# A Perceiver block's cross-attentions: the context taken by 512 keys in one piece, in place of two pieces of 256

## The chip, the cores and the metric

The kernel runs on one core of a Trainium2 chip. The metric is the device time of one execution in microseconds (us); lower is better. The core has five engines that run side by side and meet at semaphores: TensorE (PE in the profile, with its weight loads as PEld), VectorE (DVE), ScalarE (ACT), GpSimd (POOL) and SyncE (SP), which here issues the transfers between the chip's main memory and the on-chip memory SBUF. Matrix products land in a second on-chip memory, PSUM.

## The reference, cut to what matters

The model is a Perceiver of four layers on two sequences (b = 0, 1) of 256 rows and 256 features. Each layer is a cross-attention to a context of 4096 rows per sequence, then a self-attention, then a feed-forward block:

```python
x = x + _L0_xattn_ref(_layernorm(x, axis=-1), ctx_1024, mask_BxS2_bk0, ...)   # one head, masked
x = x + _L0_attn_ref(...);  x = x + _L0_ffn_ref(...)
x = x + _L1_xattn_ref(_layernorm(x, axis=-1), ctx_1024, ctx_1024, ...)        # one head
x = x + _L1_attn_ref(...);  x = x + _L1_ffn_ref(...)
x = x + _L2_xattn_ref(_layernorm(x, axis=-1), ctx_1024, ...)                  # one head
x = x + _L2_attn_ref(...);  x = x + _L2_ffn_ref(...)
x = x + _L3_xattn_ref(_layernorm(x, axis=-1), ctx_1024, mask_BxS2_ik0, ...)   # 16 heads
x = x + _L3_attn_ref(...);  x = x + _L3_ffn_ref(...)
```

The first three cross-attentions have one head of 256 features. Each is softmax(q k^T) v over 4096 keys, for 256 queries of each sequence. In layer 0 some keys are masked.

## The kernel before, in words

**One-head cross-attention** (`xattn_mean`, called by `xattn`). The key projection is folded into the queries and the value projection is done after the mean, so scores are taken straight from the context: 256 queries against the transposed context `ctxT`, and the weighted mean of the context rows `ctx`. It runs six times, for n = 0, 1, 2 and b = 0, 1. The 4096 keys are walked in 8 units of `UN` = 512 keys; a unit has two steps, one for each half q of 128 queries, so a call has 16 steps.

For exactness near fp32 every operand of a product is a pair h + l: h is the value rounded by ScalarE in a copy to fp32r, l is the rest, from a subtraction. `mm3` (L405) makes one product of a pair by a pair with three matmuls.

A unit's context comes in four transfers of 256 KB: two halves of `CK` = 256 keys of `ctxT` (L715) and two of `ctx` (L717), into buffers `raw`, of which there are 6. `parts` splits each half: h by ScalarE (L725), l by POOL (L727) or DVE (L729). The table `POOL` (L1790) says which: of the keys `kx` the first half goes to DVE and the second to POOL; of the values `vx` both go to POOL. `KV_BUFS` (L1789) gives four half-size buffers to each of `kx` and `vx`, that is two units.

Step i does the following, in this order of writing:

- `scores(i)`: splits of the next unit (keys at q = 0, values at q = 1, then the fetch of the unit after), and the score products into one PSUM bank `s`: for each half h of the keys and each half c of the features one `mm3`, so 12 matmuls of 256 columns (L405, tile xs).
- `turn(i - 1)`: four transposes of the previous step's exponentials on PE (L777), and their h part on ScalarE (L779).
- `greatest(i)`: for n = 0 a predicated copy on DVE that overwrites masked scores in PSUM (L756, with the mask `gone` and the value `fill` in SBUF), then the greatest score of each row on DVE (L758) and a running minimum of its negative (L760).
- the l part of the transposed exponentials on DVE (L780).
- `exponents(i)`: the exponential on ScalarE (L766), the scale of the older sums (L768, L771).
- `values(i - 2)`: 12 matmuls of 256 columns (L405, tile xmm<-xvx,xpT) and the running sum on DVE (L792, L793).

All these but the splits and transfers are tied by `Turns` to the order of writing on each engine. The splits, the transfers, and the work of other stages are placed among them by the framework's scheduler, which fixes one static order for each engine. Every engine and SP's queue then run in that order: an instruction that waits holds those behind it.

**What runs beside it.** There are two lanes. The x lane holds the cross-attentions; the a lane holds the self-attentions and feed-forward blocks of the other sequence, whose weights come as 128x1024 tiles (512 KB) and are split in the same way: h on ScalarE (L395), l on POOL (L397) or DVE (L399) by turns.

**Preparation for layer 3** (`prep`, `prep_alone`). Keys and values of layer 3's 16 heads are projected from the same split context and stored to main memory. `PREP` (L1785) has ten units prepared within cross-attentions, from the pieces that these hold; the other six are done by `prep_alone`, which fetches and splits pieces of 256 keys itself, with the buffers of `KV_BUFS` in its first use, ahead of the first cross-attention, and with two elsewhere.

Of the kernel before, what the change touches and what calls it, by code (L numbers as in the profile page):

```python
# [18 lines left out]
F32 = mybir.dt.float32  # L19
# [9 lines left out]
P = 128  # L29
# [603 lines left out]
class Perceiver:  # L633
# [51 lines left out]
    def xattn_mean(self, xp, n, b, queries):  # L685

        k, nc = self.x, self.nc  # L690
        masked = n == 0
        n_u, n_h, n_t = L // self.UN, self.UN // self.CK, self.UN // P
        qkT, qb, fill = queries
        ctxT = self.ins["ctxT"].rearrange("(c p) n -> p c n", p=P)
        prep = self.PREP.get((n, b), ())
        if prep:
            w3 = k.weights("x3.wk", "x3.wv")
        tie = Turns(self.tc).put
        raw, kx, vx, gone, score, exps, turned = {}, {}, {}, {}, {}, {}, {}


        least, most, total, o = ([None, None] for _ in range(4))

        def fetch(u):
            if masked:
                gone[u] = k.t(xp, [P, self.UN], "gone", U8, bufs=3)
                at = u * self.UN
                nc.sync.dma_start(gone[u], self.gone_d[b : b + 1, at : at + self.UN].to_broadcast([P, self.UN]))
            for name in ("kx", "vx"):
                raw[name, u] = []  # L710
                for h in range(n_h):
                    at = b * L + u * self.UN + h * self.CK
                    r = k.t(xp, [P, 2, self.CK], "raw", bufs=self.KV_BUFS["raw"])
                    if name == "kx":
                        nc.sync.dma_start(r, ctxT[:, :, at : at + self.CK])  # L715
                    else:
                        nc.sync.dma_start(r, self.ins["ctx"][at : at + self.CK, :].rearrange("(k p) d -> p k d", p=P))  # L717
                    raw[name, u].append(r)

        def parts(name, got, u):  # L720
            got[u] = []
            for h, r in enumerate(raw.pop((name, u))):
                both = k.t(xp, [P, 2, 2, self.CK], name, F32R, bufs=self.KV_BUFS[name])
                x = Pair(both[:, 0], both[:, 1])
                nc.scalar.copy(x.h, r)  # L725
                if self.POOL[name][h]:
                    nc.gpsimd.tensor_tensor(x.l, r, x.h.bitcast(F32), ALU.subtract)  # L727
                else:
                    nc.vector.tensor_sub(x.l, r, x.h)  # L729
                got[u].append(x)  # L730

        def scores(i):
            u, q = divmod(i, 2)
            if i == 0:
                fetch(0)
                parts("kx", kx, 0)
                parts("vx", vx, 0)
                fetch(1)
            if u + 1 < n_u:
                if q == 0:  # L740
                    parts("kx", kx, u + 1)
                else:
                    parts("vx", vx, u + 1)
                    if u + 2 < n_u:
                        fetch(u + 2)
            score[i] = k.t(k.ps, [P, self.UN], "s")
            for h in range(n_h):
                for c in range(2):
                    k.mm3(score[i][:, h * self.CK : (h + 1) * self.CK], qkT[:, c, q * P : (q + 1) * P], kx[u][h][:, c, :], c == 0, c == 1, tie)
            if q == 1 and u in prep:  # L750
                self.prep(xp, b, u, kx[u], *w3)

        def greatest(i):
            u, q = divmod(i, 2)
            if masked:
                tie(nc.vector.copy_predicated(score[i], gone[u], fill[:, q : q + 1].to_broadcast([P, self.UN])))  # L756
            nm = k.t(k.sm, [P, 1], f"nm{q}")
            tie(nc.vector.tensor_reduce(nm, score[i], axis=AX.X, op=ALU.max, negate=True))  # L758
            if u:
                tie(nc.vector.tensor_scalar(nm, nm, least[q], None, ALU.min))  # L760
            least[q] = nm

        def exponents(i):
            u, q = divmod(i, 2)
            p, su = k.t(xp, [P, self.UN], "p", bufs=2), k.t(k.sm, [P, 1], f"su{q}", bufs=4)
            tie(nc.scalar.activation(p, score.pop(i), AF.Exp, bias=least[q], accum_out=su))  # L766
            top, down = k.t(k.sm, [P, 1], f"top{q}"), None
            tie(nc.vector.tensor_scalar(top, least[q], -1.0, qb[:, q : q + 1], ALU.mult, ALU.add))  # L768
            if u:
                down = k.t(k.sm, [P, 1], f"down{q}")  # L770
                tie(nc.scalar.activation(down, top, AF.Exp, bias=most[q], scale=-1.0))  # L771
            most[q], exps[i] = top, (p, su, down)

        def turn(i):
            p, pst = exps[i][0], k.t(k.ps, [P, 512], "mm")
            for t in range(n_t):
                tie(nc.tensor.transpose(pst[:, t * P : (t + 1) * P], p[:, t * P : (t + 1) * P], self.eye))  # L777
            turned[i] = k.t2(xp, [P, self.UN], "pT", bufs=2)
            tie(nc.scalar.copy(turned[i].h, pst))  # L779
            return lambda: tie(nc.vector.tensor_sub(turned[i].l, pst, turned[i].h))  # L780

        def values(i):
            u, q = divmod(i, 2)
            (_, su, down), pT = exps.pop(i), turned.pop(i)
            acc = k.t(k.ps, [P, 512], "mm")[:, :D]
            for t in range(n_t):
                k.mm3(acc, pT[:, t * P : (t + 1) * P], vx[u][t // 2][:, t % 2, :], t == 0, t == n_t - 1, tie)
            if u == 0:
                o[q], total[q] = k.t(xp, [P, D], f"o{q}", bufs=1), su
                tie(nc.vector.tensor_copy(o[q], acc))  # L790
            else:
                tie(nc.vector.tensor_scalar(su, total[q], down, su, ALU.mult, ALU.add))  # L792
                tie(nc.vector.scalar_tensor_tensor(o[q], o[q], down, acc, ALU.mult, ALU.add))  # L793
                total[q] = su

        steps = 2 * n_u
        for i in range(steps + 2):
            rest = lambda: None
            if i < steps:
                scores(i)  # L800
            if 1 <= i <= steps:
                rest = turn(i - 1)
            if i < steps:
                greatest(i)
            rest()
            if i < steps:
                exponents(i)
            if i >= 2:
                values(i - 2)
        ps = k.mm2()  # L810
        for q in range(2):
            r = k.t(k.sm, [P, 1], "ur")
            nc.vector.reciprocal(r, total[q])
            nc.vector.tensor_scalar(o[q], o[q], r, None, ALU.mult)
            for c in range(2):
                nc.tensor.transpose(ps[:, c, q * P : (q + 1) * P], o[q][:, c * P : (c + 1) * P], self.eye)
        oT = k.t2(xp, [P, 2, S], "kvk", bufs=2)
        k.split(oT, ps)
        return oT
# [17 lines left out]
    def prep_alone(self, xp, b, units, bufs=None):  # L837
# [6 lines left out]
        for u in units:  # L844
            kx = []
            for h in range(self.UN // self.CK):
                at = b * L + u * self.UN + h * self.CK
                both = k.t(xp, [P, 2, 2, self.CK], "kx", F32R, bufs=bufs or self.KV_BUFS["kx"])
                kx.append(Pair(both[:, 0], both[:, 1]))
                raw = k.t(xp, [P, 2, self.CK], "raw", bufs=bufs or self.KV_BUFS["raw"])  # L850
                nc.sync.dma_start(raw, ctxT[:, :, at : at + self.CK])
                k.split(kx[h], raw, lo=nc.gpsimd)
            k.mm_tags = ["mm", "mm", "pr"]
# [3 lines left out]
    def prep(self, xp, b, u, kx, wk, wv, bufs=2):  # L857

        k, nc = self.x, self.nc
        for m in range(2):  # L860
            ps = k.mm()
            for h, x in enumerate(kx):
                for d in range(2):
                    k.mm3(ps[:, h * self.CK : (h + 1) * self.CK], wk[d][:, m * P : (m + 1) * P], x[:, d, :], d == 0, d == 1)
            kk = k.t2(xp, [P, self.UN], "kvk", bufs=bufs)
            k.split(kk, ps, k.col("x3.bk", m))
            for dst, part in ((self.kh_d, kk.h), (self.kl_d, kk.l)):
                nc.sync.dma_start(dst[b, u, :HD, 8 * m : 8 * m + 8, :].rearrange("d h n -> h d n"), part.bitcast(F32))
        v = k.t(xp, [P, 4, self.UN // P, GRP, HD + 1], "kvv", bufs=1)
        nc.gpsimd.memset(v[:, :, :, :, HD], 1.0)  # L870
        for h, x in enumerate(kx):
            ps = k.mm2()
            for t in range(2):
                for d in range(2):
                    k.mm3(ps[:, t, :], x[:, d, t * P : (t + 1) * P], wv[d], d == 0, d == 1)
            for t in range(2):
                k.copy(v[:, :, 2 * h + t, :, :HD], ps[:, t, :].rearrange("p (g j d) -> p g j d", g=4, j=GRP))
        nc.sync.dma_start(self.v_d[b, :, :, u, :].rearrange("g p n -> p g n"), v.rearrange("p g k j r -> p g (k j r)"))
# [907 lines left out]

    ALONE = {}
    FIRST, BEFORE, BEHIND = (0, 2), (2, 4), (4, 6)
    KV_BUFS = {"kx": 4, "vx": 4, "raw": 6}  # L1789
    POOL = {"kx": (0, 1), "vx": (1, 1)}  # L1790

    @contextmanager
    def psum(self, lane, **tags):
# [132 lines left out]
```

## Time and profile before

| what | value |
|---|---|
| median of 3 runs (lowest, highest) | 1585.57 us (1581.46, 1586.45) |
| the profiled execution's own time | 1590.7 us |
| its span, first to last instruction | 1588.9 us |
| mean granted TensorE clock | 0.916 |
| busy share of the span: PE, DVE, ACT, POOL | 87%, 70%, 56%, 34% |

The steps of the six cross-attentions, by the starts of their first and last row maximum (L758):

| call | first, us | last, us |
|---|---|---|
| n = 0, b = 0 | 35.4 | 95.1 |
| n = 0, b = 1 | 97.6 | 172.7 |
| n = 1, b = 0 | 345.8 | 472.7 |
| n = 1, b = 1 | 476.0 | 581.8 |
| n = 2, b = 0 | 603.9 | 667.2 |
| n = 2, b = 1 | 715.5 | 797.7 |

How to read the profile: times are from one execution. A row of a group has the line, the engine, the operation, the tiles written and read by the program's names, the shapes, how many there were, and their durations. Matmuls follow each other in a pipeline, so their durations overlap; what one costs in a row of them is the distance from start to start. A timeline row has the start, the length, the engine, the line and the operation, and in brackets how long the engine was idle before it and what ended that. The table of windows gives each engine's busy time in a stretch.

### The profile page before, as it was taken

The page shows a single profiled execution, that of the slowest core. Times are in us where ns is not written, and L with a number is a line of the kernel's source. Part 1 is how long each engine was busy: PE and PEld are TensorE (multiplying, and loading weights), DVE is VectorE, ACT ScalarE, POOL GpSimd, SP SyncE. Part 2 cuts the span into 40 slices and gives each one's busy share as a digit, 9 for nine tenths or more (in the row PEclk, how much of TensorE's full clock was granted, in tenths as well). Part 3 has the DMA queues.
Part 4 walks back from the last instruction along what each step waited for, and adds up shares of the span by engine and source line. Part 5 has one row for each costly group of instructions (what it writes and reads, how often), then busy time and mean ns, then how long its engine had stood idle before and what let it go on. Part 6 is the DMA issues. An engine that isn't in the chain of part 4 may idle for free.

```text
span 1588.9 us, 29546 instructions
## 1 busy us (share of the span) xinstructions
PE 1387.5 (87%) x11278; PEld 1126.0 (71%) x11278; DVE 1106.4 (70%) x1895; ACT 891.8 (56%) x1669; POOL 534.7 (34%) x395
## 2 busy tenths in 40 slices
PE   6899798978999998989973679979999999888498
PEld 6898688968899998988973245645555554774387
DVE  6999755455577787865663666759999980566764
ACT  5676455556866656745631016648888889233242
POOL 6655244444455454663354000120000000530441
PEclk9999899979999999999996558879999999996699
DMA  8753165564556575546454512456676741200471
GB/s 292 224 150 115 51 177 172 187 192 160 166 160 207 161 217 162 160 143 187 134 143 122 85 59 57 111 131 114 113 116 111 114 71 31 85 1 3 175 254 35
DMA packets 126628, 212.32 MB, mean 134 GB/s; under 512 B 14212, under 2 KB 90532, under 8 KB 122964
## 3 DMA queue, kind: packets, MB, share of 16 engines
q1 hardware_dynamic: 126488, 210.45, 48.7%
q8 instruction: 89, 1.46, 0.4%
q14 instruction: 51, 0.42, 0.1%
HBM read 181.72 MB, written 29.01 MB: 133 GB/s over the span
## 4 chain that ended last, share of the span: by engine, by line
PE 46%; DVE 16%; DMA 9%; ACT 4%; POOL 3%; issue 2%; SPq 1%; DVEq 0%; ACTq 0%; POOLq 0%
PE amm L405 9%; PE xacc L573 7%; DVE xpm L1375 6%; PE xmm L405 5%; PE xf L1369 5%; PE xs L405 4%; PE xpr L405 3%; DMA awr<-in_w 3%; PE amm L1396 2%; DMA xk<-akh_d 2%; PE xs L1396 2%; PE amm L1756 2%; PE xmm L777 1%; PE amm L573 1%; POOL aw L397 1%
## 5 line engine op out<-in xcount | busy, mean ns | idle before, releaser
L1375 DVE TENSOR_REDUCE xpm<-xf 128x2 f32<-128x1024 f32 x232 | 281.7, 1222 | 34.2 <-PE xf L1369 31.9
L397 POOL TENSOR_TENSOR aw<-awr,aw 128x1024 fp32r<-128x1024 f32 (+1 forms) x61 | 145.7, 2390 | 299.8 <-ACT aw L395 294.0
L1397 ACT ACTIVATE xp<-amm 128x512 f32<-128x512 f32 x299 | 170.1, 595 | 31.0 <-PE amm L1396 17.9
L395 ACT CAST aw<-awr 128x1024 fp32r<-128x1024 f32 (+1 forms) x114 | 115.5, 1016 | 116.0 <-DMA awr<-in_w 69.5
L405 PE MATMUL xmm<-xvx,xpT 128*128 128x256 f32 x1152 | 167.0, 291 | 4.5 <-DVE xpT L780 2.5
L573 PE MATMUL xacc<-xp,xv 128*17 128x256 f32 x2048 | 165.7, 397 | 0.9 <-DVE xot L591 0.9
L405 PE MATMUL xs<-xkx,xqkT 128*128 128x256 f32 x1152 | 164.0, 286 | 1.4 <-POOL xkx L727 0.6
L727 POOL TENSOR_TENSOR xvx<-xraw,xvx 128x512 fp32r<-128x512 f32 x96 | 131.6, 1387 | 82.9 <-ACT xvx L725 72.1
L405 PEld LDWEIGHTS xmm<-xvx,xpT 128*128 128x128 f32 x1152 | 147.7, 193 | 8.0 <-issue 3.7
L405 PEld LDWEIGHTS xs<-xkx,xqkT 128*128 128x128 f32 x1152 | 149.2, 193 | 3.5 <-POOL xkx L727 1.0
L1397 ACT ACTIVATE xp<-xs 128x512 f32<-128x512 f32 x213 | 123.5, 595 | 37.1 <-PE xs L1396 22.5
L1369 PE MATMUL xf<-xk,xq 49*128 49x512 f32 x464 | 125.4, 530 | 15.8 <-DVE xpm L1375 6.9
L1369 PEld LDWEIGHTS xf<-xk,xq 49*128 49x128 f32 x464 | 46.7, 195 | 114.4 <-issue 79.8
L399 DVE TENSOR_TENSOR aw<-awr,aw 128x1024 fp32r<-128x1024 f32 (+1 forms) x53 | 81.2, 1533 | 66.5 <-ACT aw L395 66.2
L405 PE MATMUL amm<-axnT,aw 128*128 128x256 f32 x648 | 101.1, 313 | 11.7 <-ACT axnT L395 6.9
L405 PEld LDWEIGHTS amm<-axnT,aw 128*128 128x128 f32 x648 | 92.3, 216 | 20.3 <-ACT axnT L395 9.7
L405 PE MATMUL amm<-ah,aw 128*128 128x256 f32 x768 | 99.3, 285 | 6.6 <-ACT au L1002 3.3
L1396 PE MATMUL amm<-xq,xk 51*128 51x256 f32 x598 | 99.6, 297 | 4.2 <-DVE aqT L393 2.9
L727 POOL TENSOR_TENSOR xkx<-xraw,xkx 128x512 fp32r<-128x512 f32 x48 | 72.3, 1506 | 89.8 <-ACT xkx L725 89.7
L405 PEld LDWEIGHTS amm<-ah,aw 128*128 128x128 f32 x768 | 94.3, 191 | 9.3 <-ACT au L1002 3.9
L1420 POOL TENSOR_TENSOR ax<-ax,ax 128x128 f32<-128x128 f32 x8 | 3.7, 458 | 281.8 <-DVE ax L603 281.8
L1396 PEld LDWEIGHTS amm<-xq,xk 51*128 51x128 f32 x598 | 83.9, 188 | 18.2 <-issue 12.6
(545 smaller groups left out, 2918.0 us busy)
## 6 DMA issues: line engine op xcount, KB each, us to landing
awr<-in_w SPq DMA_DIRECT2D x106, 512.0 KB
xraw<-in_ctxT SPq DMA_DIRECT2D x108, 256.0 KB
xraw<-in_ctx SPq DMA_DIRECT2D x96, 256.0 KB
xk<-akh_d SPq DMA_DIRECT2D x128, 128.0 KB
av_d<-xkvv SPq DMA_DIRECT2D x16, 544.0 KB
xv<-av_d SPq DMA_DIRECT2D x32, 272.0 KB
akh_d<-xkvk SPq DMA_DIRECT2D x32, 256.0 KB
akl_d<-xkvk SPq DMA_DIRECT2D x32, 256.0 KB
```

The source lines that it names most:

```text
L395: nc.scalar.copy(dst.h, src)
L397: lo.tensor_tensor(dst.l, src, dst.h.bitcast(F32), ALU.subtract)
L399: nc.vector.tensor_sub(dst.l, src, dst.h)
L405: tie(self.nc.tensor.matmul(out, lhsT=x, rhs=y, start=start and i == 0, stop=stop and i == 2))
L573: inst = self.nc.tensor.matmul(acc[STRIP * j : STRIP * j + v(j).shape[1], :S], lhsT=v(j), rhs=p[:, j, :], start=start, stop=stop)
L727: nc.gpsimd.tensor_tensor(x.l, r, x.h.bitcast(F32), ALU.subtract)
L777: tie(nc.tensor.transpose(pst[:, t * P : (t + 1) * P], p[:, t * P : (t + 1) * P], self.eye))
L1369: tie(nc.tensor.matmul(ps[h], lhsT=q4[rows, j, t * P : (t + 1) * P], rhs=k4[rows, j, :], start=True, stop=True))
L1375: nc.vector.tensor_reduce(at, both.rearrange("p (h n) -> p h n", h=2), axis=AX.X, op=ALU.max)
L1396: tie(nc.tensor.matmul(ps[h][:, j, :], lhsT=ks[c][rows, a + j, s * P : (s + 1) * P], rhs=q4[rows, a + j, :], start=True, stop=True))
L1397: exps = [nc.scalar.activation(p[:, h, a : a + 2, :], ps[h], AF.Exp, scale=0.25) for h in range(2)]
L1756: nc.tensor.matmul(ps[:, f, :], lhsT=w1[half][:, c, f * P : (f + 1) * P], rhs=buf[:, c, e * cap : (e + 1) * cap], start=c == 0, stop=c == 1)
```

## The change

A unit's 512 keys are one piece. There are two transfers of 512 KB for a unit in place of four of 256 KB; `raw` has 3 buffers of twice the size; each piece is split by one ScalarE copy of 128x1024 and one subtraction of 128x1024, on DVE for keys and on POOL for values, with 2 buffers of a whole unit. The score products have 512 columns: 6 matmuls a step in place of 12. `prep` takes one piece of 512 or two of 256 keys. `prep_alone` still takes pieces of 256, and its first use now has 2 buffers for splits and 3 for raw pieces, where it had 4 and 6. Line numbers after the change: scalar copy L717, POOL subtraction L719, DVE subtraction L721, predicated copy L746, row maximum L748, exponential L756.

```diff
         def fetch(u):
+            at = b * L + u * self.UN
             if masked:
...
-            for name in ("kx", "vx"):
-                raw[name, u] = []
-                for h in range(n_h):
-                    at = b * L + u * self.UN + h * self.CK
-                    r = k.t(xp, [P, 2, self.CK], "raw", bufs=self.KV_BUFS["raw"])
...
+            r = raw["kx", u] = k.t(xp, [P, 2, self.UN], "raw", bufs=3)
+            nc.sync.dma_start(r, ctxT[:, :, at : at + self.UN])
+            r = raw["vx", u] = k.t(xp, [P, 2 * self.UN], "raw", bufs=3).rearrange("p (k d) -> p k d", k=n_t)
+            nc.sync.dma_start(r, self.ins["ctx"][at : at + self.UN, :].rearrange("(k p) d -> p k d", p=P))
 
         def parts(name, got, u):
-            got[u] = []
-            for h, r in enumerate(raw.pop((name, u))):
-                both = k.t(xp, [P, 2, 2, self.CK], name, F32R, bufs=self.KV_BUFS[name])
-                x = Pair(both[:, 0], both[:, 1])
-                nc.scalar.copy(x.h, r)
-                if self.POOL[name][h]:
-                    nc.gpsimd.tensor_tensor(x.l, r, x.h.bitcast(F32), ALU.subtract)
-                else:
-                    nc.vector.tensor_sub(x.l, r, x.h)
-                got[u].append(x)
+            r = raw.pop((name, u))
+            got[u] = x = k.t2(xp, list(r.shape), name, bufs=2)
+            nc.scalar.copy(x.h, r)
+            if name == "vx":
+                nc.gpsimd.tensor_tensor(x.l, r, x.h.bitcast(F32), ALU.subtract)
+            else:
+                nc.vector.tensor_sub(x.l, r, x.h)
...
-            for h in range(n_h):
-                for c in range(2):
-                    k.mm3(score[i][:, h * self.CK : (h + 1) * self.CK], qkT[:, c, q * P : (q + 1) * P], kx[u][h][:, c, :], c == 0, c == 1, tie)
+            for c in range(2):
+                k.mm3(score[i], qkT[:, c, q * P : (q + 1) * P], kx[u][:, c, :], c == 0, c == 1, tie)
             if q == 1 and u in prep:
-                self.prep(xp, b, u, kx[u], *w3)
+                self.prep(xp, b, u, [kx[u]], *w3)
...
-                k.mm3(acc, pT[:, t * P : (t + 1) * P], vx[u][t // 2][:, t % 2, :], t == 0, t == n_t - 1, tie)
+                k.mm3(acc, pT[:, t * P : (t + 1) * P], vx[u][:, t, :], t == 0, t == n_t - 1, tie)
...
-                both = k.t(xp, [P, 2, 2, self.CK], "kx", F32R, bufs=bufs or self.KV_BUFS["kx"])
+                both = k.t(xp, [P, 2, 2, self.CK], "kx", F32R, bufs=bufs or 2)
...
-                raw = k.t(xp, [P, 2, self.CK], "raw", bufs=bufs or self.KV_BUFS["raw"])
+                raw = k.t(xp, [P, 2, self.CK], "raw", bufs=bufs or 3)
...
-                    k.mm3(ps[:, h * self.CK : (h + 1) * self.CK], wk[d][:, m * P : (m + 1) * P], x[:, d, :], d == 0, d == 1)
+                    k.mm3(ps[:, h * n : (h + 1) * n], wk[d][:, m * P : (m + 1) * P], x[:, d, :], d == 0, d == 1)
...
-    KV_BUFS = {"kx": 4, "vx": 4, "raw": 6}
-    POOL = {"kx": (0, 1), "vx": (1, 1)}
```

More of the change, by code (lines that the diff above doesn't have):

```diff
@@ L691, in xattn_mean @@
         masked = n == 0
-        n_u, n_h, n_t = L // self.UN, self.UN // self.CK, self.UN // P
+        n_u, n_t = L // self.UN, self.UN // P
         qkT, qb, fill = queries
@@ L704, in fetch @@
         def fetch(u):
+            at = b * L + u * self.UN
             if masked:
                 gone[u] = k.t(xp, [P, self.UN], "gone", U8, bufs=3)
-                at = u * self.UN
-                nc.sync.dma_start(gone[u], self.gone_d[b : b + 1, at : at + self.UN].to_broadcast([P, self.UN]))
-            for name in ("kx", "vx"):
-                raw[name, u] = []
-                for h in range(n_h):
-                    at = b * L + u * self.UN + h * self.CK
-                    r = k.t(xp, [P, 2, self.CK], "raw", bufs=self.KV_BUFS["raw"])
-                    if name == "kx":
-                        nc.sync.dma_start(r, ctxT[:, :, at : at + self.CK])
-                    else:
-                        nc.sync.dma_start(r, self.ins["ctx"][at : at + self.CK, :].rearrange("(k p) d -> p k d", p=P))
-                    raw[name, u].append(r)
-        def parts(name, got, u):
-            got[u] = []
-            for h, r in enumerate(raw.pop((name, u))):
-                both = k.t(xp, [P, 2, 2, self.CK], name, F32R, bufs=self.KV_BUFS[name])
-                x = Pair(both[:, 0], both[:, 1])
-                nc.scalar.copy(x.h, r)
-                if self.POOL[name][h]:
-                    nc.gpsimd.tensor_tensor(x.l, r, x.h.bitcast(F32), ALU.subtract)
-                else:
-                    nc.vector.tensor_sub(x.l, r, x.h)
-                got[u].append(x)
+                nc.sync.dma_start(gone[u], self.gone_d[b : b + 1, at - b * L :][:, : self.UN].to_broadcast([P, self.UN]))
+            r = raw["kx", u] = k.t(xp, [P, 2, self.UN], "raw", bufs=3)
+            nc.sync.dma_start(r, ctxT[:, :, at : at + self.UN])
+            r = raw["vx", u] = k.t(xp, [P, 2 * self.UN], "raw", bufs=3).rearrange("p (k d) -> p k d", k=n_t)
+            nc.sync.dma_start(r, self.ins["ctx"][at : at + self.UN, :].rearrange("(k p) d -> p k d", p=P))
+        def parts(name, got, u):
+            r = raw.pop((name, u))
[5 more added lines that the diff above has]
+                nc.vector.tensor_sub(x.l, r, x.h)
         def scores(i):
@@ L861, in prep @@
             ps = k.mm()
+            n = self.UN // len(kx)
             for h, x in enumerate(kx):
                 for d in range(2):
-                    k.mm3(ps[:, h * self.CK : (h + 1) * self.CK], wk[d][:, m * P : (m + 1) * P], x[:, d, :], d == 0, d == 1)
+                    k.mm3(ps[:, h * n : (h + 1) * n], wk[d][:, m * P : (m + 1) * P], x[:, d, :], d == 0, d == 1)
             kk = k.t2(xp, [P, self.UN], "kvk", bufs=bufs)
@@ L870, in prep @@
         nc.gpsimd.memset(v[:, :, :, :, HD], 1.0)
-        for h, x in enumerate(kx):
+        for h in range(2):
             ps = k.mm2()
             for t in range(2):
+                x, at = kx[(2 * h + t) * P // n], (2 * h + t) * P % n
                 for d in range(2):
-                    k.mm3(ps[:, t, :], x[:, d, t * P : (t + 1) * P], wv[d], d == 0, d == 1)
+                    k.mm3(ps[:, t, :], x[:, d, at : at + P], wv[d], d == 0, d == 1)
             for t in range(2):
```

## The prediction

> **What bounds the kernel now.** I read the engines' busy slices first, then a table of windows over the six cross-attentions, then the timeline of one unit. The 40 slices of the span and the windows say which engine sets the pace where:
>
> ```profile
> PE   6899798978999998989973679979999999888498
> DVE  6999755455577787865663666759999980566764
> ...
> 75.00:100.00 25.00, 24.00 (x199) 23.24 (x198) 22.80 (x54) 18.87 (x45) 17.33 (x12) 1.00 0.55 160
> 125.00:150.00 25.00, 22.99 (x167) 21.40 (x168) 23.27 (x48) 15.75 (x36) 15.90 (x11) 1.00 0.41 128
> 150.00:175.00 25.00, 22.56 (x171) 21.73 (x169) 23.70 (x52) 14.13 (x34) 11.07 (x8) 0.93 0.15 47
> 500.00:525.00 25.00, 25.00 (x215) 25.00 (x214) 22.23 (x48) 17.47 (x39) 14.74 (x11) 1.00 0.56 163
> 625.00:650.00 25.00, 25.00 (x213) 24.85 (x212) 20.84 (x49) 19.05 (x43) 16.36 (x12) 1.00 0.48 149
> ```
>
> (A window's columns: PE, PEld, DVE, ACT, POOL busy us, clock, DMA share, GB/s.) In the masked layer 0 (to 175 us) DVE is busy 91 to 95% of the time and PE has gaps; in layers 1 and 2 (500, 625) PE is packed and DVE has some air. So DVE work counts in the first, PE work in the second. One masked unit:
>
> ```profile
> 80.25 0.70 DVE L756 COPY_PREDICATED xs<-xgone,xfill 128x512 f32<-128x512 uint8 x1 [0.28 <-PE xs L405]
> 80.86 0.68 DVE L729 TENSOR_TENSOR xkx<-xraw,xkx 128x512 fp32r<-128x512 f32 x1
> 81.46 0.68 DVE L758 TENSOR_REDUCE xnm<-xs 128x1 f32<-128x512 f32 x1
> 82.18 0.21 DVE L760 TENSOR_SCALAR xnm<-xnm,xnm 128x1 f32<-128x1 f32 x1
> ...
> 83.60 0.90 DVE L756 COPY_PREDICATED xs<-xgone,xfill 128x512 f32<-128x512 uint8 x1
> ...
> 87.08 0.70 DVE L756 COPY_PREDICATED xs<-xgone,xfill 128x512 f32<-128x512 uint8 x1 [0.33 <-PE xs L405]
> ```
>
> ```profile
> 80.99 1.70 POOL L727 TENSOR_TENSOR xkx<-xraw,xkx 128x512 fp32r<-128x512 f32 x1 [2.13 <-ACT xkx L725]
> 82.65 2.99 POOL L727 TENSOR_TENSOR xvx<-xraw,xvx 128x512 fp32r<-128x512 f32 x2
> ```
>
> The unit lasts 87.08 - 80.25 = 6.83 us, with 0.33 us of DVE idle. The second predicated copy takes 0.90 us and not 0.70, while POOL subtracts. Two more places show what that is:
>
> ```profile
> 51.58 2.53 POOL L727 TENSOR_TENSOR xvx<-xraw,xvx 128x512 fp32r<-128x512 f32 x2 [3.06 <-ACT xvx L725]
> 53.04 1.63 DVE L756 COPY_PREDICATED xs<-xgone,xfill 128x512 f32<-128x512 uint8 x1 [1.01 <-PE xs L405]
> ...
> 652.60 1.29 POOL L727 TENSOR_TENSOR xkx<-xraw,xkx 128x512 fp32r<-128x512 f32 x1 [2.10 <-ACT xkx L725]
> 652.78 1.66 DVE L729 TENSOR_TENSOR xkx<-xraw,xkx 128x512 fp32r<-128x512 f32 x1
> ```
>
> A DVE operation with two SBUF inputs that starts while POOL subtracts ends about 0.55 us after POOL's instruction ends (54.11 to 54.67; 653.89 to 654.44): it is **held** to the end of that instruction.
>
> **PE, removed.** Per step 12 products of 256 columns become 6 of 512. Both forms stand side by side in layer 0's attention:
>
> ```profile
> 136.28 1.12 PE L405 MATMUL amm<-axrT,aw 128*128 128x256 f32 x8
> ...
> 137.24 2.00 PE L405 MATMUL amm<-aw,axrT 128*128 128x512 f32 x8
> ```
>
> With the last one's own length taken off (0.28 and 0.39 us), seven distances are 0.84 and 1.61 us: 120 and 230 ns. So a pair of 256 costs 240, one of 512 costs 230 to 232, and a step saves 6 x 8 = 0.05 us: 96 steps save 4.6 us, and the key products of `prep` in ten units 10 x 2 x 0.05 = 1.0 us. Layers 1 and 2 have 64 of the steps and all those of `prep`: 4.1 us. Where PE does not set the end it saves nothing; I take 3.
>
> The Trainium skill, "TensorE: Matmul & The Clock Gate", Back-to-back issue gap, gives a sustained 131 ns for a 512-column matmul in a stream with weight loads; by that figure my estimate would be 576 x (240 - 131) = 63 us saved. The row above shows 230 ns for just such a stream, and I go by the row.
>
> **ACT, removed.** Two casts of 128x512 (620 ns) become one of 128x1024 (L395's row has a median of 1046 ns): 96 x 0.19 = 18 us less. ACT is busy 56% of the span and under 80% in all these windows, so this is 0 on the path; below nothing it would be worth at most the waits of PE for the exponential in layer 0, 12.2 + 4.4 us by the table of waits.
>
> **DVE and POOL, moved.** The durations:
>
> ```profile
> L729 DVE TENSOR_TENSOR xkx<-xraw,xkx x48: 676/684/2800, 27.7 to 781.4; 128x512 fp32r<-128x512 f32 x48
> L399 DVE TENSOR_TENSOR aw<-awr,aw x53: 676/1226/2685, 18.4 to 1554.5; 128x1024 fp32r<-128x1024 f32 x49, 128x512 fp32r<-128x512 f32 x4
> L397 POOL TENSOR_TENSOR aw<-awr,aw x61: 1264/2398/3351, 9.4 to 1559.4; 128x1024 fp32r<-128x1024 f32 x57, 128x512 fp32r<-128x512 f32 x4
> ```
>
> The key split on DVE grows from 0.68 to 1.23 us, 0.54 a unit, 26 us in all; POOL's key split goes (48 x 1.5 us by its mean), and its two value splits of 1.29 become one of about 2.3. Two effects on holds go against each other. The key split no longer meets POOL's half of the same keys: at eleven places like 652.78 that meeting cost 0.5 to 1.1 us, 9 us together. But the value split is now one instruction: before, DVE could slip in after the first half (83.60 waited only to 83.94); after, it waits for the end of the whole.
>
> Worked out for the unit of 80.25, from those starts and the order of the changed program (predicated copy, maximum, key split, minimum on DVE; key copy, transposed part, value copy, exponential on ACT). The value buffer is now free only after all 12 value products, near 82.1, where the half was free at 81.4, so the one copy runs to 83.15 and the exponential starts there and not at 82.69: 0.46 late (DVE's longer split alone makes it about as late). POOL's value split runs from 83.15 to about 85.45. The second predicated copy, ready at about 84.1, is held to 85.45 and ends near 86.0, where it ended at 84.50: 1.5 late. PE has 0.5 of slack before the transposes that follow, and part of the first delay is in the second. The unit comes to 7.7 us: **+0.9**. From DVE's side: 6.5 busy + 0.54 + a hold of 1.3 in place of 0.2 is 8.1 if nothing overlaps, 7.0 if no hold is longer than before. I keep +0.2 and +1.3 as ends, and take 0.9, as the order of the two queues gives it.
>
> Sum for layer 0: b = 0 has four such units (66 to 96 us), 3.6; in the four before, which other work stretches to about 8 us, I take the bare 0.5: 2.0. b = 1 lasts ten us a unit, DVE 93% busy: 0.8 each, 6.4. Together **+12** (ends 3 and 21, by 16 x 0.2 and 16 x 1.3).
>
> Layers 1 and 2, 32 units: no predicated copy, so the long value split finds fewer DVE operations to hold; +0.54 a unit on DVE, less the 7 of the 9 us that lie here. If DVE set the end, 32 x 0.54 - 7 = +10; if the meetings alone counted, -7. PE is packed there and covers most; I take +2, and without that cover it is the +10.
>
> **Transfers and the start.** SP issues half as many, of 512 KB. A key transfer now waits for the whole key split; it then has about 4.9 us to land before its copy on ACT, much as before (81.57 to 86.36), but carries twice the bytes. If late, ACT stands, and the transposed part and the exponential queue behind it. The nearest row is L725's wait for in_ctxT: 6.8 us in three. Range -1 to +16 (0.5 a unit in layers 1 and 2); I take 0. With 2 and 3 buffers the first `prep_alone` serializes with its products; the first scores come later, but the first predicated copy (34.67) comes after both in either order: +1, from -2 to +4.
>
> **Sum:** +12 - 3 + 2 + 0 + 1 = +12 us on the profiled execution's 1590.7 (span 1588.9, 1.8 around it), 1602.7. That execution stands 5.1 above the median of the runs; on 1585.6 it is **1597.5 us**.
>
> **Rivals.**
> *Held less than it gains (faster, 1578 us).* The meetings on the key split vanish and PE's rows shorten. For it: 9 us of meetings, and that most predicated copies after 100 us already face POOL. Price: -5.6 (all PE) -7 (meetings in layers 1 and 2) +5 (layer 0: 16 x 0.3, bare growth with fewer holds) = -8. It decides if the predicated copy's mean stays at or under 0.97 us, its mean now.
> *Nothing (1587 us).* Layer 0 loses 5, the rest gains 4: one delay absorbed in the slack of 0.5 a unit.
> *Late transfers (1615 us).* +0.5 a unit in 32 units, 16, on top of +12: the profile has DMA share 0.5 to 0.6 there, with weight tiles of 512 KB in the same queues. Against: the wait is seldom now.
> That the change does not do what it says is out: the changed order has 576 score products of 512 columns.
>
> **Chances.** Forecast 0.52, late transfers 0.18, nothing 0.16, faster 0.14. A measurement tells 0.3% (4.8 us) from no change: faster 0.14, same 0.16, slower 0.70. Range 1580 to 1616: it leaves out the lower half of the faster case and the upper part of the late one; the forecast's own is 1591 to 1607.
>
> **What would show it.** Right: steady masked units near 7.7 us, predicated copies (L746) with a mean near 1.4 us and every second one ending with POOL's L719; L721 at 1.2 us, 48 times, rarely longer; xs matmuls 230 ns apart; layers 1 and 2 as long as before. Wrong: units still at 6.8 to 7.0; or ACT copies (L717) that wait for in_ctxT in layers 1 and 2; or the stretch from 175 to 345 us taking up the delay, if it has slack that the windows hide.

## The result, and the profile after

The changed kernel takes 1597.26 us (median of 10 runs, 1590.24 to 1602.91) beside 1585.17 us for the kernel before (10 runs): a ratio of 1.0074, 95% interval 1.0049 to 1.0100. It is slower, and by as much as was forecast (1597.5 us). The profiled execution has a span of 1601.0 us beside 1588.9.

First the slices of the span after the change, then the windows that the prediction read (columns as there):

```profile
PE   6888888969998999979985489989999999888498
DVE  5998865537577777975664476768999990467765
```

```profile
75.00:100.00 25.00, 21.35 (x137) 17.74 (x136) 24.41 (x47) 15.79 (x32) 7.13 (x3) 1.00 0.54 154
...
150.00:175.00 25.00, 24.18 (x152) 21.67 (x153) 21.86 (x48) 15.56 (x32) 9.72 (x6) 1.00 0.32 93
500.00:525.00 25.00, 22.48 (x138) 20.45 (x139) 20.80 (x45) 16.42 (x33) 11.73 (x7) 0.87 0.57 160
625.00:650.00 25.00, 24.14 (x171) 21.87 (x170) 21.41 (x46) 18.85 (x38) 11.21 (x6) 1.00 0.46 148
```

From 75 to 100 us DVE is busy 24.41 of 25 us and PE has 21.35: in the masked layer DVE is even more the engine that sets the pace than before. One masked unit, DVE and then POOL:

```profile
90.44 0.69 DVE L746 COPY_PREDICATED xs<-xgone,xfill 128x512 f32<-128x512 uint8 x1
91.16 0.69 DVE L748 TENSOR_REDUCE xnm<-xs 128x1 f32<-128x512 f32 x1
91.77 1.22 DVE L721 TENSOR_TENSOR xkx<-xraw,xkx 128x1024 fp32r<-128x1024 f32 x1
...
93.93 0.47 DVE L783 SCALAR_TENSOR_TENSOR xo<-xo,xdown,xmm 128x256 f32<-128x256 f32 x1
94.31 2.10 DVE L746 COPY_PREDICATED xs<-xgone,xfill 128x512 f32<-128x512 uint8 x1
96.44 0.69 DVE L748 TENSOR_REDUCE xnm<-xs 128x1 f32<-128x512 f32 x1
...
98.59 0.69 DVE L746 COPY_PREDICATED xs<-xgone,xfill 128x512 f32<-128x512 uint8 x1
```

```profile
93.48 2.37 POOL L719 TENSOR_TENSOR xvx<-xraw,xvx 128x1024 fp32r<-128x1024 f32 x1 [5.78 <-ACT xvx L717]
```

The unit lasts 98.59 - 90.44 = 8.15 us, where it lasted 6.83. The second predicated copy takes 2.10 us and not 0.69: it starts 0.83 us after POOL's instruction and ends at 96.41, 0.56 after POOL's end at 95.85. No DVE row from 89 to 100 us carries a bracket, so DVE never waits for another engine's result there: the time is in the length of its own instructions. In the whole kernel 32 predicated copies are above 0.70 us by 17.0 us in sum, where they were by 8.8 (those of more than 0.80 us counted); of the 13 held ones, eleven end 0.55 or 0.56 us after a value split of POOL.

The holding goes both ways. In one place of the masked layer DVE's key split was ahead (it starts at 69.62 us, POOL's value split at 69.80): there POOL's split lasts 3.90 us in place of 2.37, and the predicated copy that follows on DVE at 70.75 takes its plain 0.69 us.

In the windows of layers 1 and 2, at 500 and 625 us, PE is busy 22.48 and 24.14 of 25 us, where it had all of them.

Where the 12.1 us of span came from, by the starts of the first and last row maximum of the six cross-attentions, in the two profiled executions:

| stretch | before, us | after, us | difference |
|---|---|---|---|
| start to the first row maximum | 35.4 | 40.9 | +5.5 |
| layer 0, b = 0, first to last | 59.7 | 66.6 | +6.9 |
| between the two | 2.4 | 3.8 | +1.3 |
| layer 0, b = 1 | 75.1 | 78.1 | +3.0 |
| from there to the last one of layer 2 | 625.0 | 621.9 | -3.1 |
| the rest, which the change does not touch | 791.3 | 789.8 | -1.5 |

### The profile page after: what moved, and what is told of

It reads as the page before. It is cut to its first block, busy times and chain, and to the rows that moved or that the text cites. A ratio compares the mean times of both kernels' runs of the same rounds, so it can differ in the third digit from the quotient of the medians.

```text
span 1601.0 us, 27626 instructions
## 1 busy us (share of the span) xinstructions
PE 1389.7 (87%) x10582; PEld 1091.2 (68%) x10582; DVE 1124.8 (70%) x1895; ACT 883.6 (55%) x1573; POOL 455.2 (28%) x299
## 4 chain that ended last, share of the span: by engine, by line
PE 46%; DVE 18%; DMA 7%; ACT 4%; issue 2%; POOL 2%; SPq 0%; DVEq 0%; ACTq 0%; POOLq 0%
PE amm L405 10%; DVE xpm L1367 7%; PE xacc L573 6%; PE xmm L405 5%; PE xf L1361 4%; PE xs L405 4%; PE xpr L405 3%; PE amm L1388 2%; DMA xk<-akh_d 2%; PE xs L1388 2%; PE amm L1748 2%; PE xmm L767 1%; DMA awr<-in_w 1%; DVE xpm L1365 1%; PE amm L573 1%
## 5 line engine op out<-in xcount | busy, mean ns | idle before, releaser
L719 POOL TENSOR_TENSOR xvx<-xraw,xvx 128x1024 fp32r<-128x1024 f32 x48 | 119.2, 2482 | 177.9 <-ACT xvx L717 157.0
L405 PE MATMUL xs<-xkx,xqkT 128*128 128x512 f32 x576 | 156.9, 405 | 4.6 <-DVE xkx L721 2.1
L405 PEld LDWEIGHTS xmm<-xvx,xpT 128*128 128x128 f32 x1152 | 152.0, 198 | 6.1 <-DVE xo L783 1.7
L405 PEld LDWEIGHTS xs<-xkx,xqkT 128*128 128x128 f32 x576 | 104.9, 195 | 22.7 <-DVE xkx L721 2.4
L1388 PEld LDWEIGHTS amm<-xq,xk 51*128 51x128 f32 x598 | 84.1, 190 | 15.7 <-issue 12.6
L756 ACT ACTIVATE xp<-xs,xnm 128x512 f32<-128x512 f32 x96 | 66.4, 691 | 39.3 <-DVE xnm L750 37.2
```

The lines of the kernel that those rows point to most:

```text
L405: tie(self.nc.tensor.matmul(out, lhsT=x, rhs=y, start=start and i == 0, stop=stop and i == 2))
L1388: tie(nc.tensor.matmul(ps[h][:, j, :], lhsT=ks[c][rows, a + j, s * P : (s + 1) * P], rhs=q4[rows, a + j, :], start=True, stop=True))
```

## The experiments

Ratios are to runs of the kernel before on the same chip; the changed kernel's own is 1.0074 (1.0049 to 1.0100), and 1.0094 (1.0059 to 1.0129) in the last group. Differences between two kernels are also given in us of medians where both ran in one group. Theory H is the prediction's: in layer 0 the one long value split of POOL holds DVE's predicated copy. The rivals are K (the longer key split on DVE), S (the later start), T (whole buffers and transfers). A steady unit is one of the last units of the first call, where little other work shares the engines.

**The value split in two halves.**

```diff
-                nc.gpsimd.tensor_tensor(x.l, r, x.h.bitcast(F32), ALU.subtract)
+                for j in (slice(0, 2), slice(2, 4)):
+                    nc.gpsimd.tensor_tensor(x.l[:, j], r[:, j], x.h[:, j].bitcast(F32), ALU.subtract)
```

> The changed kernel with one edit: POOL subtracts the value piece in two instructions of 128x512 in place of one of 128x1024. Theory H (the long value split holds the predicated copy of layer 0; the profile of the changed kernel shows 94.31 to 96.41 us for a copy that takes 0.69 alone, ending 0.56 us after POOL's instruction): the copy is let in after the first half, the hold falls from about 1.4 us to 0.2 to 0.8, the steady masked unit falls from 8.15 us to 7.3 (end 7.0 to 7.6), the predicated copies' mean from 1.25 us to about 0.95, and the kernel is faster by 16 x 0.6 = 10 us, at about 1588. Rival K (layer 0 pays for the longer key split on DVE, 1.22 in place of 0.68 us, and not for the hold): unit and time stay, 1597 within 2. Rival S (the later start, 5.5 us to the first row maximum, is the main loss): stays in both, and the time moves under 2 us.

Measured: 1585.79 us, 0.9988 (0.9959 to 1.0017). The static order is nearly that of the changed kernel: 18 of the 3468 instructions of DVE and ScalarE stand elsewhere. Its steady unit on DVE, and POOL:

```profile
90.80 0.97 DVE L747 COPY_PREDICATED xs<-xgone,xfill 128x512 f32<-128x512 uint8 x1
...
94.13 0.70 DVE L747 COPY_PREDICATED xs<-xgone,xfill 128x512 f32<-128x512 uint8 x1
...
98.01 0.98 DVE L747 COPY_PREDICATED xs<-xgone,xfill 128x512 f32<-128x512 uint8 x1
```

```profile
89.95 2.97 POOL L720 TENSOR_TENSOR xvx<-xraw,xvx 128x512 fp32r<-128x512 f32 x2 [4.23 <-ACT xvx L717]
```

The unit is 98.01 - 90.80 = 7.21 us, the held copy waits 0.27 and not 1.41 us, and the copies are above 0.70 us by 6.6 us in sum (17.0 with the one long split). POOL's work has not become less, 2.97 us for the two; only the piece that DVE must wait out is shorter. The whole loss of the change is gone with this one edit. In the profiles the last row maximum of layer 0 comes at 178.9 us in place of 189.4. The key split is still one of 1.22 us on DVE here and the first row maximum still late, at 41.6 us, so K and S as the main cause fall; H stands. A steady unit stays 0.38 us above the 6.83 of before. In layers 1 and 2, where no predicated copy is, nothing moved: 622.0 us from the end of layer 0 to the end of layer 2, beside 621.9.

**The keys half on POOL again, the value split long.**

```diff
-                nc.vector.tensor_sub(x.l, r, x.h)
+                j, g = slice(0, self.CK), slice(self.CK, self.UN)
+                nc.vector.tensor_sub(x.l[:, :, j], r[:, :, j], x.h[:, :, j])
+                nc.gpsimd.tensor_tensor(x.l[:, :, g], r[:, :, g], x.h[:, :, g].bitcast(F32), ALU.subtract)
```

> The changed kernel with one edit: the low part of the keys again half on DVE and half on POOL, 128x512 each, from the one piece of 512; the value split stays one POOL instruction. Theory H: the hold by the value split stays, so the steady masked unit falls only by the part of 0.54 us of DVE that lies outside the hold: 7.6 to 8.1 us, and the predicated copies' mean stays at 1.2 us or above; the meetings of the two halves of the keys come back. Time 1593 (1590 to 1597). Rival K: 16 x 0.54 = 9 us come back in layer 0, 1588.

Measured: 1616.70 us, 1.0155 (1.0111 to 1.0200), 5 runs. The steady unit is 8.16 us and the copies' mean 1.20 us, so in the steady unit the hold is as H says and K gives nothing back. The first call as a whole is shorter, 60.8 us beside 66.6, by its first units, where the order has moved; and the time is 20 us over the upper end that H gave, and further from K. So this run decides little. Part of the loss is a new collision. Both halves now wait for one ScalarE copy, so they are ready in the same moment; DVE's half, then POOL's:

```profile
L722 DVE TENSOR_TENSOR xkx<-xraw,xkx x48: 680/1014/2548, 35.1 to 812.8; 128x512 fp32r<-128x512 f32 x48
L723 POOL TENSOR_TENSOR xkx<-xraw,xkx x48: 1276/1736/2245, 36.5 to 812.5; 128x512 fp32r<-128x512 f32 x48
```

Their medians were 684 and 1360 ns before, when two copies on ScalarE staggered them. The rest lies mainly in a first row maximum at 44.9 us and in a stretch between layer 0 and layer 1 of 186.9 us (175.3 in the changed kernel), where no context piece of the changed form is split and the static order had moved. Why that stretch grew stays open.

**Both edits: all splits as before.** The two edits above together.

> The changed kernel with both edits: keys half on DVE and half on POOL, values in two POOL instructions of 128x512, as in the kernel before; what stays of the change is the one transfer, the one ScalarE copy, the whole buffers, the 512-column score products and the fewer buffers at the start. Theory H with the start: layer 0's steady unit within 0.3 us of the 6.83 us of before, the time that of before, plus 4 to 5 us of start, less 3 to 5 us of the score products in layers 1 and 2: 1586 (1582 to 1590). Rival T (whole buffers, freed late, and the transfers cost as much as the splits): the unit stays over 7.4 us and the time over 1592.

Measured: 1600.18 us, 1.0068 (1.0040 to 1.0095); steady units (from row maximum to row maximum) of 7.02 and 7.06 us with one of 8.63 between. Their mean, 7.57, is more than H allowed (within 0.3 of 6.83) and lies in T's branch, as the time does, 14 us over the forecast of H. Against the run above the value halves are worth 16.5 us again. What is left, 13 us over the kernel before by medians, does not lie in layer 0's calls, which last 59.1 and 74.0 us where they lasted 59.7 and 75.1; the start is at 45.2 us where it was at 35.4. The last experiment takes this up.

**The key term alone, in the kernel before.**

```diff
-    POOL = {"kx": (0, 1), "vx": (1, 1)}
+    POOL = {"kx": (0, 0), "vx": (1, 1)}
```

> The kernel before with one edit in its table: both halves of the keys are subtracted on DVE (two of 128x512, 1.3 us a unit in place of 0.68), none on POOL; values stay in two POOL instructions. It is the key term alone, without the long value split. Theory H: layer 0's units gain up to 0.3 us (DVE is longer by 0.6, the meetings with POOL's half of the keys go, 0.5 to 1.1 us where they occurred), layers 1 and 2 within 5 us of before: time 1586 (1581 to 1591). Rival K: 16 x 0.6 = 10 us in layer 0 and some in layers 1 and 2: 1595 or more.

Measured: 1587.17 us, 1.0003 (0.9974 to 1.0031). The steady unit does grow, to 7.61 us (+0.78, more than the 0.3 expected), yet the time stays, and K's 1595 did not come. This is not the key term alone, though: a fifth of DVE's instructions stand elsewhere in the static order. In the profile, of an execution 11 us over the median, layer 0 ends at 187.7 us in place of 172.7; its second call lasts 89.6 us beside 75.1, with more of the other lane's work in it (PE is busy 77.0 us there, 67.9 before), and 9.6 us come back by the end of layer 2. What the longer key split costs in layer 0 by itself is not shown.

**The score products in 256 columns again.**

```diff
             for c in range(2):
-                k.mm3(score[i], ..., kx[u][:, c, :], c == 0, c == 1, tie)
+            for h in (slice(0, self.CK), slice(self.CK, self.UN)):
+                for c in range(2):
+                    k.mm3(score[i][:, h], ..., kx[u][:, c, h], c == 0, c == 1, tie)
```

> The changed kernel with one edit: the score products of a step are again 12 of 256 columns in place of 6 of 512, from the same one piece; all else stays. It is the PE term alone. Theory H (the prediction's price): 0.05 us a step come back, 4.6 us in 96 steps, of which those in layers 1 and 2 count: 1600 (1597 to 1603); in the trace products of 256 columns start 120 ns apart and the steady masked unit stays at 8.1 us, since DVE sets it. Rival N (the form of the products is worth nothing, PE has air elsewhere): 1597 within 2. A gain of 10 us or more would say that the wide products cost something that the profile of the changed kernel hides.

Measured: 1598.55 us, 1.0097 (1.0069 to 1.0124). Against the changed kernel's ratio that is +0.0023, 3.6 us, on the side that was expected; but the intervals overlap, 1598.55 lies within rival N's 2 us of 1597 too, and the static order moved much, so the time does not show the term (the steady unit stays at 8.15 us, as expected). The pitch does. The twelve narrow products of this run, and then the six wide ones of the changed kernel:

```profile
90.40 1.60 PE L405 MATMUL xs<-xkx,xqkT 128*128 128x256 f32 x12
```

```profile
92.11 1.55 PE L405 MATMUL xs<-xkx,xqkT 128*128 128x512 f32 x6
```

With the last one's own length taken off (0.28 and 0.39 us), eleven distances are 1.32 and five are 1.16 us: 120 and 232 ns, 1.44 and 1.39 us a step. The gain is 0.05 us a step, as priced.

**The start.** The first preparation for layer 3 puts its two halves into one buffer of the full size, so there is again room for four halves of splits and six of raw pieces:

```diff
+            if bufs is None:
+                whole, wide = k.t2(xp, [P, 2, self.UN], "kx", bufs=2), k.t(xp, [P, 2, self.UN], "raw", bufs=3)
...
+                if bufs is None:
+                    j = slice(h * self.CK, (h + 1) * self.CK)
+                    kx.append(Pair(whole.h[:, :, j], whole.l[:, :, j]))
+                    raw = wide[:, :, j]
```

> The changed kernel with one edit: the first preparation for layer 3 puts its two halves of 256 keys into one buffer of the full size, so that its first use again has room for four halves of splits and six of raw pieces. It is the start term alone. Theory S (fewer buffers let the planner put the sixth weight copy, which stands 4.3 us for its transfer, ahead of the first key copy): the first row maximum comes at 36 us (35 to 38) in place of 40.9, and the kernel is faster by 4 to 6 us, 1592. Rival A (the later start is absorbed by the other lane's work further on): the first row maximum comes early as well, the time stays at 1597 within 2.

Measured: 1595.03 us, 1.0053 (1.0021 to 1.0085). ScalarE at the start, in the changed kernel and then in this one:

```profile
32.03 1.05 ACT L395 CAST aw<-awr 128x1024 fp32r<-128x1024 f32 x1 [4.32 <-DMA awr<-in_w]
32.99 1.04 ACT L717 CAST xkx<-xraw 128x1024 fp32r<-128x1024 f32 x1
```

```profile
27.72 1.05 ACT L717 CAST xkx<-xraw 128x1024 fp32r<-128x1024 f32 x1
28.67 0.38 ACT L383 COPY xkvv<-xmm 128x256 f32<-128x256 f32 x1
28.93 1.06 ACT L395 CAST aw<-awr 128x1024 fp32r<-128x1024 f32 x1
```

In the changed kernel the first key copy stands behind two weight copies, at 22.97 and 32.03 us, and the second of them waits 4.3 us for its transfer; with the room given back it goes ahead of both, and the first row maximum comes at 35.9 us. The queue order is shown; in time the two intervals overlap, so the last group repeated the pair on one chip:

> The changed kernel unaltered, timed beside the three others of this group on one chip, so that the start and the splits can be read as differences within a group: 1.007 times the kernel before.

> The changed kernel with the first preparation in full-size buffers once more (the edit of e6_start_buffers), beside the changed kernel itself. Theory S: 5 us less than the changed kernel (3 to 8; in the profiles the last row maximum of the second cross-attention came 7 to 11 us earlier). Rival A (absorbed by the other lane): within 2 us of it.

Measured: 1603.17 us, 1.0094 (1.0059 to 1.0129), and 1596.51 us, 1.0041 (1.0016 to 1.0065): 6.7 us apart. Four pairs differ in the start alone: these two, 6.7 us; the changed kernel and this edit by their ratios in the earlier groups, 3.3; the value halves without and with it (next experiment), 0.2; all splits as before without and with it (last experiment), 7.3. Their mean is 4.4 us. S is supported as a second, smaller cause of about that size, but beside the value halves it does not show, and no pair of intervals is apart.

**Both edits that help.** The start's room and the value halves:

> The changed kernel with two edits: the first preparation in full-size buffers, and the value piece subtracted in two POOL instructions of 128x512. If the two terms add up (11.5 us measured for the value halves, 4 to 6 us expected for the start): 1581 (1578 to 1584), which is faster than the kernel before by 0.2 to 0.5%. If the start is absorbed: 1586.

Measured: 1580.66 us, 0.9987 (0.9956 to 1.0018), in one group with the start's edit alone at 1595.03: the value halves are worth 14.4 us here, 10 by the ratios. The median is the one forecast, but the kernel before stood at 1582.74 in this group, and by the ratio the start adds nothing to the value halves (0.9988 without it). Taken with both edits, the rest of the change is worth nothing that the interval can tell.

**A second profile of the changed kernel.**

> The changed kernel once more, unaltered, for a second profile: it tells how far a stage's length may be trusted. The steady masked unit should repeat within 0.05 us, the stretch from the first to the last row maximum of the first two cross-attentions within 1 us, and the rest follow the granted clock; a stage that moves by more than 2 us between two profiles of one kernel carries no conclusion.

Measured: a span of 1591.4 us beside 1601.0. The steady unit repeats at 8.15, the first call at 66.1 us (66.6); the second call has 75.1 and 78.1. So the +3.0 of the second call in the table above carries no conclusion, and the same goes for the smaller terms behind layer 0.

**The value split in quarters.** With the start's room:

```diff
-                nc.gpsimd.tensor_tensor(x.l, r, x.h.bitcast(F32), ALU.subtract)
+                for j in range(4):
+                    nc.gpsimd.tensor_tensor(x.l[:, j], r[:, j], x.h[:, j].bitcast(F32), ALU.subtract)
```

> The changed kernel with the first preparation in full-size buffers and the value piece subtracted in four POOL instructions of 128x256. Theory H (an operation of DVE is held to the end of the one POOL instruction that runs): holds get shorter again, the predicated copies' mean falls from 0.91 to 0.98 us (halves) to 0.85 or less, the steady masked unit from 7.21 to 7.0 us, and the time to 12 to 16 us under the changed kernel. Rival P (more instructions cost POOL as much as they free): the unit at 7.2 us or more and the time as with halves, 11 to 16 us under.

Measured: 1577.12 us, 0.9939 (0.9907 to 0.9971): faster than the kernel before and 26 us under the changed kernel in the same group, more than either theory gave. It is the fastest version here. The steady unit is still 7.2 us and the copies' mean 0.92 us, where H forecast 7.0 and 0.85 or less, so the gain is not where H put it; DVE's timeline of this kernel:

```profile
84.05 1.12 DVE L747 COPY_PREDICATED xs<-xgone,xfill 128x512 f32<-128x512 uint8 x1
...
87.38 0.70 DVE L747 COPY_PREDICATED xs<-xgone,xfill 128x512 f32<-128x512 uint8 x1
...
91.27 1.12 DVE L747 COPY_PREDICATED xs<-xgone,xfill 128x512 f32<-128x512 uint8 x1
```

The held copy is even a little longer (1.12 beside 0.98): it starts 0.85 us after POOL in both kernels, and then the second quarter runs, which ends 1.42 us after POOL's start, where the first half ends after 1.27. The second call is shorter, 69.7 us beside 73.1 with halves, and the copies are above 0.70 by 7.0 us (9.0 with halves and the same start). Against the halves (0.9987) the intervals overlap; why quarters should gain more is not settled.

**All splits and the start as before,** of the change only the transfer, the one copy, the whole buffers and the wide products:

> The changed kernel with the first preparation in full-size buffers, the values in two POOL instructions and the keys half on DVE and half on POOL: all splits and the room at the start as in the kernel before, and of the change only the one transfer, the one ScalarE copy, the whole buffers and the 512-column products. If the 13 us that the same splits lost without the room at the start came from the start (first row maximum at 45.2 us in place of 35.4), it is within 4 us of the kernel before. If they came from the two halves of the keys, which now get ready together and so collide (POOL's half has a median of 1.74 us in place of 1.36, DVE's 1.05 in place of 0.68), it stays 8 us or more above it.

Measured: 1589.48 us, 1.0022 (0.9996 to 1.0048), 1.7 us over the kernel before. Of the 10.8 us that the same splits lost by the ratio without the room at the start, 7.3 went with it (1.0068 to 1.0022). The first branch holds, and T falls as a main cause: with the wide products counted in, whole buffers and transfers of 512 KB cost at most 8 us by the interval. The steady units swing between 6.8 and 8.7 us, and the collision of the halves (1.13 us in the mean on DVE) is still there, so part of the remaining 1.7 may be that.

## Why the prediction was right, step by step

- **The sum** was +12 us, on 1585.6; measured +12.1 by medians. Its largest term is the right one, shown by the value halves. That the sum came out to 0.1 us is luck: layer 0 was put too high, at +12 where its two calls together lost 6.3 to 10.2 us in three profiles, the start too low, at +1 where it was 5.5 to 6.8, and they cancel.
- **The hold in layer 0** (+12 with the key split): the hold is shown. Three pairs of programs differ in the one or two POOL instructions alone; taking the long split apart gives 0.0086, 0.0066 and 0.0087 of the time, 14, 10 and 14 us. The price of a unit was low and the number of units high. Steady units went to 8.15 us, +1.32, where I had +0.9: POOL's split started 3.04 us after the first copy (2.90 worked out) and the held copy ended 5.97 after it (5.75), and of the 0.6 us that I let the second half-unit win back (1.5 late, +0.9 in all) only 0.4 came (2.18 us from the copy's end to the next unit, 2.58 before), because DVE's own row of operations fills it. Against that, 11 copies were held by a value split and not 16, and the units of b = 1 lost 0 to 0.4 us each, by three profiles, where I took 0.8.
- **The key split on DVE**: 1216 ns in the middle and 48 times, as said. Put into the kernel before it left the time as it was (1.0003), in a much changed order, while the steady unit grew by 0.78 us. Of the changed kernel's +1.32 a steady unit, the value halves take back 0.94; the 0.38 that stays is no more than the 0.54 that I counted, but how much of it is the key split's was not separated.
- **PE** (-3): the pitch is 232 ns against 2 x 120, as read from the row of the kernel before. The time moved 3.6 us the expected way when it was undone, within the intervals' overlap, so the 3 us are not shown. The 131 ns that the Trainium skill gives ("TensorE: Matmul & The Clock Gate", Back-to-back issue gap) was not seen in this form either, on 576 such products; the trace decides for 232.
- **Layers 1 and 2** (+2, ends -7 and +10): from the end of layer 0 to the end of layer 2 the profile lost 3.1 us, PE's term included, where PE and this one made -1. A second profile of the same kernel differs by 2.9 there, so this is agreement and no more. One step of the working is a little off: the seven meetings that lie in these layers add up to 6.1 us, not 7.
- **The start** (+1, from -2 to +4): mis-sized. The first row maximum came 5.5 us later, outside the range given, and giving the room back took 0.2 to 7.3 us off the time. I looked at the preparation's own chain and held that the first predicated copy comes "after both in either order". What I did not read was the changed order of ScalarE's queue, in which two more weight copies had moved ahead of the first key copy, one of them with a wait of 4.3 us.
- **Transfers** (0): ScalarE's key copy waits 7.5 us for its transfer in five places, 6.8 in three before; its value copy 6.3 us and 0.7. The late-transfer rival, 16 us, did not come. (Its price on top of the forecast's 12 makes 1613.6 us and not 1615.)
- **The faster rival** was to decide at a mean of the predicated copy of 0.97 us. It is 1.23 us; with the value halves it is 0.91 and the loss is gone. The sign was well chosen.

The Trainium skill states the mechanism ("SBUF — State Buffer", Who interferes with whom): DVE's second port pair is GpSimd's, and taking it is an exclusive lock. The traces agree for operations of DVE with two inputs in SBUF: the eleven held predicated copies of the changed kernel end 0.55 or 0.56 us after POOL's instruction of about 2.4 us, those of the kernel with quarters as long after one of 0.74, and the running sum at 93.93 us (one tile in SBUF, one in PSUM) takes its 0.47 us in the middle of POOL's split. That the cause is a shared port no run here can show; that DVE waits is shown.

## What to carry to other kernels

In this kernel a subtraction on POOL was also a closed door for DVE's operations with two SBUF inputs, shut for the length of one instruction: merging two POOL instructions into one held the predicated copy for 1.41 us in place of 0.27, though POOL's total fell from 2.97 to 2.37 us. Shorter is not always better: with quarters the hold in the steady unit was 0.42 us. So before pieces are made larger, look which engine sets the pace in each stage and which of its instructions can start while the longer one runs. And when buffers of a shared tag become fewer, read the new static order of every queue at the place where they are first used: here the third and fourth pieces of the first preparation were copied at 23.9 and 25.6 us, where it had been 11.9 and 12.6, and then an instruction of another lane had taken the place ahead.

## What the runs showed that I had not expected

- Ten runs of the changed kernel spread from 1590 to 1603 us, and the granted clock goes with most of it: 0.921 goes with 1590.9 and 0.911 with 1602.1. Within each kernel that had ten runs or more, 0.01 less mean clock goes with 9 to 14 us more. Between kernels the mean clock differs too, 0.920 for the kernel before and 0.912 to 0.915 for the changed one. In the start window from 34 to 66 us, where PE's busy time fell from 25.8 to 23.8 us, the clock is 0.84 after and 1.00 before. The late start does not make it by itself: with the room given back it is 1.00, with the room and the value halves 0.84. Whether gaps on PE lower the clock, and so return a stall a second time, or the other way round, these runs do not settle.
- Two halves of one piece, given to DVE and POOL by one releasing copy, took longer than staggered ones: 1.01 and 1.74 us in the middle, where it had been 0.68 and 1.36.
- Four POOL instructions of 128x256 take 3.26 us together in the steady unit, beside 2.37 for one of 128x1024, and the kernel with them is the fastest of all those run.
